# A two-thread decoder kernel: the second thread's first state-space block is prepared inside the first thread's first layer

## The chip, the core and the metric

The kernel runs on one core of a Trainium2 chip. The metric is the device time of one execution in microseconds. The core has five engines with instruction queues of their own, each worked off in order: PE (TensorE; its weight loads are listed as PEld), DVE (VectorE), ACT (ScalarE), POOL (GpSimd) and SP (SyncE, which here issues most DMAs). An instruction that waits holds up everything behind it in its engine's queue.

## The reference, cut to what matters

A decoder of 12 layers runs on x of shape (8, 256, 256), float32, each layer as `x = x + layer(layernorm(x), ...)`. The layer that the change touches is the first, a selective state-space model with a forward and a backward direction. For u after a causal convolution of four taps and a Silu it computes, per direction,

```
dbc   = u @ Wx.T                     # 64 columns dt, 16 columns B, 16 columns C
delta = softplus(dt @ Wdt.T + bdt)
h     = exp(delta * A) * h + delta * B * u      # over t, 512 channels x 16 states
y     = sum_n h * C_n + u * D
```

and then gates y with a Silu and projects it. The second layer, cross attention with 16 heads of 64 between x and a context (77 rows per batch entry), and a mixture of experts, which needs a zeroed table of slots in DRAM, follow.

## The kernel before

x is held on chip in four blocks of two batch entries each. Two threads of work share the engines: the left one takes blocks 0 and 1, the right one blocks 2 and 3, each through all 12 layers. A thread is a Python generator; `build` always advances the thread whose planned time is the smaller (`thread` adds a planned share per step, `FIRST` for the left thread's first layer), and the right thread starts at `lag`, just after the left thread's first layer. A scheduler then orders each engine's instructions, with the order of emission as priority. So the order in all queues is fixed when the program is built.

The left thread's first layer is written apart from the right's. It is `wide` (class `Wide`): it uses the buffers of both sides, and handles 512 channels of a block at once. For each of its two blocks it makes a pass in direction f and one in direction b (`way`): 16 states, each in two halves of two channel groups, so 64 scans (L829) per pass. For each of these ACT makes exp into PSUM (L825), POOL the input product db (L827), DVE the scan. For three states out of four the sum over states goes through PE transposes (L854, `ht`), an ACT scaling (L856, `ys`) and transposes back into the four sums y (L859); for every fourth state DVE multiplies by C (L832, `hc`, two buffers) and PE adds it up (L833). Between the halves `way` takes one step each from `parts`, a list of preparations: `gates` (W_in and Silu of the gate branch, L873), `channels` of the next block (norm, turn, W_in, convolution as four matmuls with diagonal `taps` and Silu, L726), `rows` (Wx matmul, copy `dbc`, store of the B and C rows to DRAM, and a small turned copy `cols`, L762), `delta` (softplus, L782) and `gated` (gate and projection of the block before, L885). In block 0's b direction the list holds all of block 1's preparation; in block 1's b direction it holds `gates` alone. Then `gated` closes the layer.

The right thread's first layer is `ssm` (L541). It loads the same weights w0 again (three DMAs, L547), and for each block normalizes and turns x, makes u (W_in, ACT copy, convolution on DVE at L565 and L569, Silu), `dbc` and `rows`. For its first block it also calls `cleared`, which zeroes the right thread's table of slots by one DMA from a zeroed tile (L902). Then it runs four passes of 32 scans (L623) per block: two channel groups at a time, both directions. Each state loads one broadcast tile `rep` (L614, 512 KB, three buffers).

Beside `ssm` the left thread runs `perceiver16`, its second layer: weights w1 (four DMAs), `joined` (norms; kv at L435), v by six matmul groups through one PSUM bank, then 8 head pairs for each batch entry with q, k, scores (`sc`, L403), softmax, transposes and `av`. SP's queue at the seam holds, in this order: w1, a context load, w0 for the right thread, the zeroes, a context load, the rows stores of block 2, the rep loads.

Of the kernel before, what the change touches and what calls it, by code (L numbers as in the profile page):

```python
# [18 lines left out]
C = 77  # L19
# [276 lines left out]
class Base:  # L296
# [22 lines left out]
    def load(self, blk):  # L319
        xd = self.d["x"].rearrange("b (i p) c -> p (b i) c", p=128)  # L320
        self.nc.sync.dma_start(self.x[blk], xd[:, 4 * blk : 4 * blk + 4, :])

    def load_rest(self):
        for blk in range(1, NB):
            self.load(blk)


class Net:
# [21 lines left out]
        self.ps = {k: pool(k, n, space=PSUM) for k, n in psum.items()}  # L350
        return es

    def weights(self, i, split=1):

        src = self.d[f"w{i}"]
        n = src.shape[1]
        m = self.d[f"r{i}"].shape[1] if f"r{i}" in self.d and src.dtype != U8 else 0
        t = self.work.tile([128, n + m], src.dtype, name=f"w{i}")
        step = -(-n // split)
        for j in range(0, n, step):  # L360
            e = min(n, j + step)
            self.nc.sync.dma_start(t[:, j:e], src[:, j:e])
# [149 lines left out]
def context(base, room, net):  # L512


    nc = net.nc
    rows = room.work.tile([C, B, D], F32, name="rows")
    nc.sync.dma_start(rows, net.d["ctx"].rearrange("b s c -> s b c"))
    yield
    for kind in ("raw", "nrm"):
        if kind == "nrm":  # L520
            net.norm([rows[:, b, :] for b in range(B)], rows, rows=C)
            yield
        dst = room.work.tile([128, 2, B * C], F32, name="turned")
# [17 lines left out]
def ssm(net):  # L541
# [2 lines left out]
    nc = net.nc  # L544
    with net.scope(mm=2, y=1):
        work = net.work
        w = net.weights(0, 3)  # L547
        neg_a, skip = {}, work.tile([128, 4], F32, name="skip")
        for d in "fb":
            e = work.tile([128, 4, 16], F32, name=f"nega_{d}")  # L550
# [2 lines left out]
            neg_a[d] = e  # L553
        nc.vector.tensor_tensor(skip, w["fD"], w["bD"], ALU.add)
        for blk in net.blks:
            xt = net.normed_turned(blk, bufs=1)
            u = work.tile([128, 4, 2, S], F32, name="u")
            for c in range(4):
                ps = net.bank()
                net.mms(ps, [(w["W_in"][:, k, c * 128 : c * 128 + 128], xt[:, k, :]) for k in range(2)])  # L560
                u0 = work.tile([128, 2, 3 + S], F32, name="u0", bufs=2)
                nc.gpsimd.memset(u0[:, :, 0:3], 0.0)
                nc.scalar.copy(u0[:, :, 3:], pairs_of(ps))
                acc = work.tile([128, 2, S], F32, name="acc", bufs=2)
                nc.vector.tensor_scalar(  # L565
                    acc, u0[:, :, 0:S], w["conv"][:, c, 0:1], w["b_conv"][:, c : c + 1], ALU.mult, ALU.add
                )
                for k in range(1, 4):
                    nc.vector.scalar_tensor_tensor(  # L569
                        acc, u0[:, :, k : k + S], w["conv"][:, c, k : k + 1], acc, ALU.mult, ALU.add  # L570
                    )
                nc.scalar.activation(u[:, c], acc, AF.Silu)
                yield
            dbc, rows = {}, {}
            for d in "fb":
                ps = net.bank()
                net.mms(pairs_of(ps[:96]), [(w[d + "Wx"][:, c, :], u[:, c]) for c in range(4)])
                dbc[d] = work.tile([96, 512], F32, name="dbc_" + d)
                nc.scalar.copy(dbc[d], ps[:96])

                rows[d] = net.base.dram.tile([32, 512], F32, name=f"rows{blk}{d}")
                nc.sync.dma_start(rows[d], dbc[d][64:96])
            if blk == net.blks[0]:
                yield from cleared(net, net)
            yield
            for c0 in range(0, 4, 2):
                y = [net.ps["y"].tile([128, 512], F32, name=f"y{c}") for c in range(2)]
                for d in "fb":
# [23 lines left out]
                    for n in range(16):  # L612
                        rep = work.tile([128, 2, 512], F32, name="rep", bufs=3)
                        nc.sync.dma_start(rep, by_state[n : n + 1].to_broadcast([128, 2, 512]))  # L614
                        for c in range(2):

                            st = net.bank()
                            nc.scalar.activation(  # L618
                                st, dl[:, c, :], AF.Exp, scale=neg_a[d][:, c0 + c, n : n + 1]
                            )  # L620
                            db = work.tile([128, 512], F32, name="db", bufs=3)
                            nc.gpsimd.tensor_tensor(db, du[:, c, :], rep[:, 0], ALU.mult)  # L622
                            nc.vector.tensor_tensor_scan(  # L623
                                st[:, order], st[:, order], db[:, order], 0.0, ALU.mult, ALU.add
                            )
                            hc = work.tile([128, 512], F32, name="hc", bufs=4)
                            nc.vector.tensor_tensor(hc, st, rep[:, 1], ALU.mult)  # L627
                            nc.tensor.matmul(  # L628
                                y[c],
                                lhsT=net.ident,  # L630
                                rhs=hc,
                                start=d == "f" and n == 0,
                                stop=d == "b" and n == 15,
                            )
                            yield
                for m in range(2):
                    c = c0 + m
                    ps = net.bank()
                    cols = slice(512 + c * 128, 640 + c * 128)
                    net.mms(ps, [(w["W_in"][:, k, cols], xt[:, k, :]) for k in range(2)])  # L640
                    res = work.tile([128, 2, S], F32, name="res")
                    nc.scalar.activation(res, pairs_of(ps), AF.Silu)
                    nc.vector.scalar_tensor_tensor(
                        u[:, c], u[:, c], skip[:, c : c + 1], pairs_of(y[m]), ALU.mult, ALU.add
                    )
                    nc.vector.scalar_tensor_tensor(u[:, c], res, 0.5, u[:, c], ALU.mult, ALU.mult)
                yield
            for b in range(2):
                net.project(blk, b, u[:, :, b], w["W_out"])
                yield  # L650


class Wide:
# [7 lines left out]

    def steps(self):
        net, nc, other = self.net, self.nc, self.other
        with net.scope(y=1), other.scope(st=2, ht=2):
            net.ps.update(other.ps)
            net.alias = {"mm": "ht"}
            near = net.work
            self.w = w = net.weights(0, 3)
            taps = near.tile([128, 4, 4, 128], F32, name="taps")
            nc.sync.dma_start(taps.rearrange("p c k m -> p (c k m)"), net.d["taps"])  # L670
            self.taps = taps
# [14 lines left out]
            for n, blk in enumerate(net.blks):  # L686
                then = {"blk": blk + 1}
                self.y = [net.ps["y"].tile([128, 512], F32, name=f"y{c}") for c in range(4)]
                for d in "fb":
                    parts = []  # L690
                    if d == "f":
# [3 lines left out]
                            parts.append(self.rows(now, "b"))  # L695
                        parts.append(self.delta(now, "b"))
                        if n == 0:
                            parts += [context(self.base, other, net)]
# [13 lines left out]
    def way(self, o, d, parts):  # L712
# [10 lines left out]
        for _ in parts:  # L723
            yield

    def channels(self, o, first=False):  # L726
# [4 lines left out]
        xt = o["xt"] = near.tile([128, 2, 512], F32, name="xt", bufs=2)  # L731
# [6 lines left out]
        u = o["u"] = near.tile([128, 4, 2, S], F32, name="u", bufs=2)  # L738
# [23 lines left out]
    def rows(self, o, d):  # L762
# [5 lines left out]
        dbc = o["dbc"][d] = near.tile([96, 512], F32, name="dbc_" + d, bufs=2)  # L768
# [1577 lines left out]
```

## Time and profile before

| | us |
|---|---|
| median of 3 runs (lowest, highest) | 4766.82 (4752.45, 4772.51) |
| profiled execution: time, span | 4753.15, 4751.4 |
| leading layer: first scan, last scan, gate | 49.2, 517.1, 520.3 |
| directions f and b of block 0, f and b of block 1, first to last scan | 107.5, 133.9, 121.5, 96.5 |
| left thread's layer 1: weights issued, first kv, first scores | 530.7, 548.8, 589.0 |
| right thread's first scan, 129th scan, last scan's start | 589.1, 977.5, 1304.8 |

The scans of each layer are counted in the timeline of DVE (64 for each direction of the left layer, 32 for each pass of the right). In a line of the timeline the first number is the start, the second the length; "x2" merges two neighbours, and brackets give the engine's idle time before it and what ended that. Line numbers are those of the listing above.

### The profile page before, as it was taken

What the parts mean: (1) busy time and instruction counts of PE and PEld (TensorE: products, weight loads), DVE (VectorE), ACT (ScalarE), POOL (GpSimd) and SP (SyncE); (2) the same over time, 40 slices, a digit from 0 to 9 for tenths busy, and PEclk for the clock granted to TensorE, in tenths of its full rate; (3) what the DMA queues carried; (4) which work ended last, traced back from release to release, by engine and by line L of the source; (5) the groups of instructions that cost most, each with busy time, mean ns of one, the idle gap of its engine ahead of it and who ended that gap; (6) DMA issues with size and microseconds to landing.
All of it is one profiled execution on the core that took longest, in us unless ns stands there. A gap on an engine that the chain in (4) does not pass through costs nothing.

```text
span 4751.4 us, 54874 instructions
## 1 busy us (share of the span) xinstructions
PE 4087.7 (86%) x20192; PEld 2663.6 (56%) x20192; DVE 2665.2 (56%) x5064; ACT 2004.2 (42%) x4513; POOL 1576.2 (33%) x1373
## 2 busy tenths in 40 slices
PE   7777788887889899988989998788989999877988
PEld 3555433433347566655766665555556767645655
DVE  6768787767841444556254556665473562243355
ACT  6767465656533343432333342422343342233331
POOL 5758454344512411124442333432011001122123
PEclk8989899988989899998989998777889999988999
DMA  3111343233416100001610000100010000001000
GB/s 125 55 33 48 117 112 101 58 90 96 99 57 235 60 1 1 13 3 71 242 42 1 1 32 16 41 14 1 1 47 1 14 36 1 34 25 40 2 18 36
DMA packets 96319, 239.72 MB, mean 50 GB/s; under 512 B 8395, under 2 KB 36403, under 8 KB 85683
## 3 DMA queue, kind: packets, MB, share of 16 engines
q1 hardware_dynamic: 86355, 179.49, 12.2%
q0 software_dynamic: 9696, 56.72, 3.4%
q8 instruction: 160, 2.62, 0.2%
q14 instruction: 108, 0.88, 0.1%
HBM read 216.05 MB, written 20.14 MB: 50 GB/s over the span
## 4 chain that ended last, share of the span: by engine, by line
PE 46%; DVE 11%; POOL 5%; issue 4%; ACT 3%; DMA 1%; POOLq 0%; DVEq 0%; ACTq 0%
PE mm L395 22%; PE sc L395 5%; PE sc L403 5%; PE av L403 3%; PE pt L395 3%; PE o L395 3%; PE mm L983 1%; DVE xn L418 1%; PE mm L403 1%; PE mm L2175 1%; PE mm L428 1%; PE mm L1840 1%; DVE hn_sq L1897 1%; DVE pex L979 1%; POOL m_part L1596 1%
## 5 line engine op out<-in xcount | busy, mean ns | idle before, releaser
L622 POOL TENSOR_TENSOR db<-du,rep 128x512 f32<-128x512 f32 x256 | 320.2, 1271 | 182.6 <-DMA rep<-rows3f 44.2
L827 POOL TENSOR_TENSOR db<-du,rep 128x512 f32<-128x512 f32 x256 | 320.9, 1284 | 105.1 <-DVE h L829 81.9
L387 ACT COPY pv<-mm 111x384 f32<-111x384 f32 (+2 forms) x387 | 197.7, 512 | 331.6 <-PE mm L983 144.6
L395 PE MATMUL mm<-xt,w 128*128 128x512 f32 (+1 forms) x704 | 310.2, 569 | 30.7 <-issue 6.2
L623 DVE TENSOR_TENSOR_SCAN mm<-mm,db 128x512 f32<-128x512 f32 x256 | 310.7, 1222 | 36.7 <-ACT mm L618 20.9
L1333 POOL TENSOR_TENSOR qs<-q,w 128x256 f32<-128x256 f32 x256 | 155.4, 628 | 479.6 <-PE sc L395 479.0
L403 PE MATMUL sc<-k,q 64*128 64x333 f32 (+1 forms) x1152 | 249.5, 492 | 74.0 <-ACT pex L970 36.1
L628 PE MATMUL y<-hc,consts 128*128 128x512 f32 x512 | 279.1, 651 | 38.0 <-DVE hc L627 37.9
L403 PE MATMUL av<-pv,v 111*64 111x256 f32 (+5 forms) x2752 | 255.6, 384 | 16.3 <-ACT pv L387 9.2
L395 PE MATMUL sc<-k,qs 128*128 128x256 f32 x1024 | 265.8, 388 | 3.4 <-ACT ex L1347 1.6
L983 PEld LDWEIGHTS mm<-consts,pex 128*111 128x111 f32 x960 | 146.2, 195 | 195.5 <-issue 52.6
L983 PE MATMUL mm<-consts,pex 128*111 128x128 f32 x960 | 197.0, 316 | 61.8 <-ACT pex L977 18.5
L829 DVE TENSOR_TENSOR_SCAN h<-st,db 128x512 f32<-128x512 f32 x192 | 223.2, 1208 | 41.4 <-ACT st L825 34.4
L395 PE MATMUL mm<-h,sw 128*128 128x256 f32 x1024 | 243.3, 384 | 0.0
L970 ACT ACTIVATE pex<-sc,pnm 128x333 f32<-128x333 f32 x320 | 170.3, 537 | 139.3 <-DVE pnm L966 122.9
L403 PEld LDWEIGHTS sc<-k,q 64*128 64x128 f32 (+1 forms) x1152 | 111.8, 200 | 195.4 <-ACT pex L970 67.9
L395 PE MATMUL mm<-kv,w 128*128 128x256 f32 (+1 forms) x640 | 207.3, 445 | 13.3 <-ACT q L1024 10.8
L416 POOL TENSOR_TENSOR rs<-ve,neghalf 128x4 f32<-128x4 f32 (+1 forms) x57 | 59.2, 1039 | 476.3 <-DVE ve L414 395.1
L395 PEld LDWEIGHTS mm<-h,sw 128*128 128x128 f32 x1024 | 192.7, 193 | 32.9 <-issue 6.9
L395 PEld LDWEIGHTS mm<-xt,w 128*128 128x128 f32 x704 | 133.6, 206 | 136.4 <-issue 82.1
L395 PE MATMUL mm<-w,ao 128*128 128x256 f32 x768 | 197.5, 398 | 12.4 <-DVE x L462 10.8
L395 PEld LDWEIGHTS sc<-k,qs 128*128 128x128 f32 x1024 | 181.7, 192 | 45.2 <-issue 15.9
(482 smaller groups left out, 9073.4 us busy)
## 6 DMA issues: line engine op xcount, KB each, us to landing
rep<-rows2f SPq DMA_DIRECT2D x32, 512.0 KB
rep<-rows2b SPq DMA_DIRECT2D x32, 512.0 KB
rep<-rows3f SPq DMA_DIRECT2D x32, 512.0 KB
rep<-rows3b SPq DMA_DIRECT2D x32, 512.0 KB
w<-in_w SPq DMA_DIRECT2D x12, 1024.0 KB
w<-in_w SPq DMA_DIRECT2D x8, 1025.0 KB
w<-in_w SPq DMA_DIRECT2D x6, 1001.0 KB
w<-in_w SPq DMA_DIRECT2D x6, 838.0 KB
```

The lines of the kernel that those rows point to most:

```text
L387: self.nc.scalar.copy(out, in_)
L395: self.nc.tensor.matmul(out, lhsT=lhs, rhs=rhs, start=n == 0, stop=n == len(pairs) - 1)
L403: self.nc.tensor.matmul(out, lhsT=lhs, rhs=rhs, start=start, stop=stop, tile_position=at)
L416: nc.gpsimd.tensor_tensor(rs[:rows], ve[:rows], self.neghalf[:rows, :n], ALU.pow)
L622: nc.gpsimd.tensor_tensor(db, du[:, c, :], rep[:, 0], ALU.mult)
L623: nc.vector.tensor_tensor_scan(st[:, order], st[:, order], db[:, order], 0.0, ALU.mult, ALU.add)
L628: nc.tensor.matmul(y[c], lhsT=net.ident, rhs=hc, start=d == "f" and n == 0, stop=d == "b" and n == 15,)
L827: nc.gpsimd.tensor_tensor(db, du[:, c, :], self.rep[:, 0], ALU.mult)
L829: nc.vector.tensor_tensor_scan(h[:, order], st[:, order], db[:, order], 0.0, ALU.mult, ALU.add)
L970: nc.scalar.activation(ex[:, e, :], sc[:, e, :NK], AF.Exp, bias=nm[:, e : e + 1], accum_out=sm[:, e : e + 1])
L983: nc.tensor.transpose(pt[:CH, j * 128 : j * 128 + 128], ex[:, e, j * CH : (j + 1) * CH], net.ident)
L1333: nc.gpsimd.tensor_tensor(qs[:, kc].rearrange("p n (h t) -> p n h t", h=H), q[:, kc, t0 : t0 + 16].rearrange("p (n t) -> p n t", n=2).unsq ...
```

## The change

Four things move together. (1) A pool `shared`, opened by the leading layer at the bottom of the right side, holds w0 and stays open until `ssm` ends, so `ssm` loads no weights. (2) In block 1's b direction the list of preparations now also holds `channels` and both `rows` of block 2, with their results in `shared`; `rows` leaves out the turned copy `cols` for it. (3) `ssm` takes these results for its first block and starts with the softplus; its second block is prepared as before. (4) `cleared` for the right thread is called after the first pass of the first block instead of ahead of it. The context rows take the buffer of `res`, since memory is needed for `shared`. `ssm` has four steps fewer, which moves the right thread's later instructions ahead by 6.5 units of the plan's 2241.

```diff
+    def hand(self):
+        self.handed = ExitStack()
+        self.shared = self.handed.enter_context(
+            self.tc.tile_pool(name="shared", bufs=1, side="right", reuse_waits="tile")
+        )
...
-    def weights(self, i, split=1):
+    def weights(self, i, split=1, pool=None):
...
-        t = self.work.tile([128, n + m], src.dtype, name=f"w{i}")
+        t = (pool or self.work).tile([128, n + m], src.dtype, name=f"w{i}")
...
-    rows = room.work.tile([C, B, D], F32, name="rows")
+    rows = net.work.tile([128, 4, 512], F32, name="res").rearrange("p a (n c) -> p (a n) c", c=D)[:C]
...
 def ssm(net):
-        w = net.weights(0, 3)
+        shared, first = net.base.shared, net.base.first
+        w = first["w"]
...
         for blk in net.blks:
+            if blk == net.blks[0]:
+                xt, u, dbc, rows = (first[k] for k in ("xt", "u", "dbc", "rows"))
+            else:
...
-            if blk == net.blks[0]:
-                yield from cleared(net, net)
             yield
             for c0 in range(0, 4, 2):
...
+                    if blk == net.blks[0] and not c0 and d == "f":
+                        yield from cleared(net, net)
...
+    net.base.handed.close()
...
 class Wide:
     def steps(self):
+        self.base.hand()
...
-            self.w = w = net.weights(0, 3)
+            self.w = w = net.weights(0, 3, self.base.shared)
...
                     else:
                         parts.append(self.gates(now))
+                        parts += [self.channels(then), self.rows(then, "f"), self.rows(then, "b")]
                         if blk != net.blks[-1]:
-                            parts += [self.channels(then), self.rows(then, "f"), self.rows(then, "b")]
                             parts.append(self.delta(then, "f"))
...
+            self.base.first = dict(now, w=w)
             self.turn(4)
...
     def rows(self, o, d):
...
         nc.sync.dma_start(rows, dbc[64:96])
         yield
+        if o["blk"] not in net.blks:
+            return
```

In the lines that are left out, `channels` and `rows` take their tiles xt, u and dbc from `shared` for a block of the other thread (one buffer) and from their own pool otherwise (two buffers), and the body of `ssm`'s preparation is indented under the `else`.

More of the change, by code (lines that the diff above doesn't have):

```diff
@@ L555, in ssm @@
         for blk in net.blks:
[L556 to L570, printed above, removed]
-                    )
-                nc.scalar.activation(u[:, c], acc, AF.Silu)
-                yield
@@ L574, in ssm @@
[L574 to L582, printed above, removed]
-            if blk == net.blks[0]:
-                yield from cleared(net, net)
+            if blk == net.blks[0]:
+                xt, u, dbc, rows = (first[k] for k in ("xt", "u", "dbc", "rows"))
+            else:
+                xt = shared.tile([128, 2, 512], F32, name="xt")
+                net.turned(net.normed(blk), [xt[:, kc, :] for kc in range(2)])
+                u = shared.tile([128, 4, 2, S], F32, name="u")
+                for c in range(4):
+                    ps = net.bank()
+                    net.mms(ps, [(w["W_in"][:, k, c * 128 : c * 128 + 128], xt[:, k, :]) for k in range(2)])
+                    u0 = work.tile([128, 2, 3 + S], F32, name="u0", bufs=2)
+                    nc.gpsimd.memset(u0[:, :, 0:3], 0.0)
+                    nc.scalar.copy(u0[:, :, 3:], pairs_of(ps))
+                    acc = work.tile([128, 2, S], F32, name="acc", bufs=2)
+                    nc.vector.tensor_scalar(
+                        acc, u0[:, :, 0:S], w["conv"][:, c, 0:1], w["b_conv"][:, c : c + 1], ALU.mult, ALU.add
+                    )
+                    for k in range(1, 4):
+                        nc.vector.scalar_tensor_tensor(
+                            acc, u0[:, :, k : k + S], w["conv"][:, c, k : k + 1], acc, ALU.mult, ALU.add
+                        )
+                    nc.scalar.activation(u[:, c], acc, AF.Silu)
+                    yield
+                dbc, rows = {}, {}
+                for d in "fb":
+                    ps = net.bank()
+                    net.mms(pairs_of(ps[:96]), [(w[d + "Wx"][:, c, :], u[:, c]) for c in range(4)])
+                    dbc[d] = shared.tile([96, 512], F32, name="dbc_" + d)
+                    nc.scalar.copy(dbc[d], ps[:96])
+                    rows[d] = net.base.dram.tile([32, 512], F32, name=f"rows{blk}{d}")
+                    nc.sync.dma_start(rows[d], dbc[d][64:96])
@@ L697, in steps @@
                         if n == 0:
-                            parts += [context(self.base, other, net)]
+                            parts.append(context(self.base, other, net))
                             parts += [cleared(Net(self.base, net.blks, side), other) for side in CLEARED]
@@ L724, in way, with of, bufs @@
             yield
+    def of(self, o):
+        return self.net.work if o["blk"] in self.net.blks else self.base.shared
+    def bufs(self, o):
+        return 2 if o["blk"] in self.net.blks else 1
     def channels(self, o, first=False):
@@ L730, in channels @@
         yield
-        xt = o["xt"] = near.tile([128, 2, 512], F32, name="xt", bufs=2)
+        xt = o["xt"] = self.of(o).tile([128, 2, 512], F32, name="xt", bufs=self.bufs(o))
         for kc in range(2):
@@ L737, in channels @@
             yield
-        u = o["u"] = near.tile([128, 4, 2, S], F32, name="u", bufs=2)
+        u = o["u"] = self.of(o).tile([128, 4, 2, S], F32, name="u", bufs=self.bufs(o))
         for c in range(4):
@@ L767, in rows @@
         net.mms(pairs_of(ps[:96]), [(w[d + "Wx"][:, c, :], o["u"][:, c]) for c in range(4)])
-        dbc = o["dbc"][d] = near.tile([96, 512], F32, name="dbc_" + d, bufs=2)
+        dbc = o["dbc"][d] = self.of(o).tile([96, 512], F32, name="dbc_" + d, bufs=self.bufs(o))
         nc.scalar.copy(dbc, ps[:96])
```

## The prediction

> **What bounds the kernel now.** I read the page's totals first, then a table of 5 us windows around the seam between the two layers, then the timeline of that seam, then the same timeline inside the leading layer, where the trace already holds a twin of the moved work.
>
> ```profile
> PE 4087.7 (86%) x20192; PEld 2663.6 (56%) x20192; DVE 2665.2 (56%) x5064; ACT 2004.2 (42%) x4513; POOL 1576.2 (33%) x1373
> ```
>
> PE is the busiest engine, but 86% is an average over stages. In the windows (columns: stretch, length, busy us of PE, PEld, DVE, ACT, POOL, granted PE clock, DMA share, GB/s) the seam is the weakest place:
>
> ```profile
> 505.00:510.00 5.00, 4.28 (x33) 3.76 (x32) 3.83 (x5) 4.81 (x9) 4.39 (x5) 0.92 0.02 3
> ...
> 525.00:530.00 5.00, 4.91 (x22) 4.02 (x23) 1.69 (x4) 0.00 (x0) 0.00 (x0) 1.00 0.00 0
> ...
> 535.00:540.00 5.00, 0.19 (x1) 0.18 (x1) 4.21 (x20) 0.00 (x0) 1.01 (x1) 0.50 0.97 392
> ```
>
> In the first row, before the leading layer ends, DVE, ACT and POOL are at 77% or more; in the second ACT and POOL stand still; in the third the DMAs are full with three transfers at once and PE's clock is granted at 0.50. The timeline says who comes back when:
>
> ```profile
> 520.29 1.41 DVE L889 SCALAR_TENSOR_TENSOR u<-u,skip,y 128x512 f32<-128x512 f32 x2 [2.03 <-PE y L859]
> 530.74 1.97 SPq L362 DMA_DIRECT2D w<-in_w  x4
> 548.84 0.81 DVE L435 TENSOR_SCALAR kv<-mm,w 128x512 f32<-128x512 f32 x1
> 588.99 1.48 PE L403 MATMUL sc<-k,q 64*128 64x333 f32 x4 [0.81 <-ACT k L387]
> 589.09 1.23 DVE L623 TENSOR_TENSOR_SCAN mm<-mm,db 128x512 f32<-128x512 f32 x1 [1.25 <-POOL db L622]
> ```
>
> The leading (left) thread needs 68.7 us from its gate (520.29) to its first score matmul (588.99), and the second (right) thread starts its first scan at the same moment (589.09). Behind that, the left thread sets the pace: the score matmuls of successive head pairs start at
>
> ```profile
> 611.59 0.83 PE L403 MATMUL sc<-k,q 64*128 64x333 f32 x4 [0.91 <-ACT k L387]
> 634.51 0.83 PE L403 MATMUL sc<-k,q 64*128 64x333 f32 x4
> ...
> 908.47 0.83 PE L403 MATMUL sc<-k,q 64*128 64x333 f32 x4
> ...
> 929.40 0.83 PE L403 MATMUL sc<-k,q 64*128 64x333 f32 x4
> ```
>
> The first gap, 22.9 us, holds 12 scans of the right thread; the second, 20.9 us, holds none. A scan of the right thread costs the left chain (22.9 - 20.9)/12 = 0.17 us, though it holds DVE for 1.22 + 0.69 us. That row decides my sign.
>
> **The change, part by part.**
>
> *Moved into the last direction (left path).* The trace has the twin: the other block's b direction prepares block 1 by the same lines 726 to 780, and in the built program the changed direction has PE's instructions in the same order. Each direction has 64 scans. Here are the 17th scan and the 49th of both, and between them the two DVE waits that the twin has:
>
> ```profile
> 181.16 2.34 DVE L829 TENSOR_TENSOR_SCAN h<-st,db 128x512 f32<-128x512 f32 x2 [0.23 <-ACT st L825]
> 218.81 0.69 DVE L832 TENSOR_TENSOR hc<-st,rep 128x512 f32<-128x512 f32 x1 [10.66 <-PE y L833]
> 260.15 0.69 DVE L832 TENSOR_TENSOR hc<-st,rep 128x512 f32<-128x512 f32 x1 [12.51 <-PE y L833]
> 262.60 1.22 DVE L829 TENSOR_TENSOR_SCAN h<-st,db 128x512 f32<-128x512 f32 x1 [1.75 <-ACT st L825]
> ...
> 443.55 2.34 DVE L829 TENSOR_TENSOR_SCAN h<-st,db 128x512 f32<-128x512 f32 x2 [0.23 <-ACT st L825]
> ...
> 495.60 2.34 DVE L829 TENSOR_TENSOR_SCAN h<-st,db 128x512 f32<-128x512 f32 x2 [0.23 <-ACT st L825]
> ```
>
> 262.60 - 181.16 = 81.4 us against 495.60 - 443.55 = 52.1 us: 29.4 us for channels and rows. (The gates stand in both, the softplus of L784 in neither.) The changed kernel leaves out the two small transpose rounds of L773 to L779, about 2 us each (249.55 to 250.4 and a bank's turn). I take **+25 us**. Upper end 37.4, the whole difference of the two directions from first scan to last (133.9 - 96.5), softplus included. Lower end 15, ACT's added instructions alone: 4 copies of 0.58, 4 Silus of 0.69, 3 copies of 0.59 and 6 table loads of 1.28 (L758 has 3, the way back to Exp 3 more) are 14.5. Nothing hides it: all four engines are at 78% to 86% in the window 405 to 520, and the wait is PE's order, in which the tap matmuls stand before y<-hc, with DVE's hc (two buffers) and everything after it in DVE's queue behind.
>
> A rule speaks against this place. The Trainium skill, "ScalarE: Activation LUTs", section "What ACT_TABLE_LOAD costs", counts about 2.66 us for every change of table set, load and drain; the six added loads would be 16 us of ACT by it. The trace has 1283 ns loads with the next ACTIVATE at once behind them (load at 240.56, Silu at 241.86), so it shows no drain after the load, and 7.7 us by its own rows.
>
> *Removed from the seam.* The right thread's weight load (3 x 838 KB, some 6.5 us of full DMA at the 392 GB/s of the window), its norm and turn, 8 W_in and 8 Wx matmuls (32 records of about 0.45 = 14.4 us of PE, at 555 to 580 where PE is full) and 4 x 0.55 + 12 x 0.75 = 11.2 us of DVE convolution. The convolution comes back as 16 tap matmuls, inside the +25.
>
> *Right thread.* Its first Abs needs only the prepared projection: PE's first Wdt matmul follows the last y turn directly. From Abs to first scan takes 589.09 - 578.51 = 10.6 us now; behind the gate's DVE work (to 525.4) I get about 533 + 25 = **558 us instead of 589**, 31 us earlier.
>
> *Left thread in the seam.* In DVE's built order 6 scans (1.22), 6 products (0.69) and the softplus (about 3) now stand before kv: 14.5 us; some is waiting now, so kv moves from 548.84 to 562 before the shift, +13. POOL's powers for the norms wait behind six db of 1.27, which is how those us come about. After kv the 14.4 us of PE are gone, less what the right thread's matmuls add: -13. PE's half clock in 535 to 555 covers 7.6 us of busy time and can give back 3.8. I take **0**, bounds -10 and +10. First left score matmul: 589 + 25 = **614**.
>
> *SP's queue.* The rows stores (64 KB each) and cleared's zeroing move. Though cleared stands later in the text, SP gets it before the left thread's layer-1 weights: three rep loads (1.5 MB) and 2.94 MB of zeros, together 1.5/0.17 + 2.94/0.39 = 16 us by the rates of the windows 580 to 585 (rep loads alone) and 535 to 540, start about 10 us before those 4.2 MB. They are needed at kv, 30 us after their issue; 6 + 11 us fit under DVE's work. Cover gone, up to 7 us. The ctx rows' new home in res costs nothing: gates needs it at 179, the last reader is done at 118.
>
> *What the lead is worth.* In the built program 17 y matmuls of the right thread stand before the first left score matmul (none now), but at the 128th scan 48 score matmuls against 52, at the 256th 108 against 112: the lead shrinks to one head pair, 21 us. Left gains 17 x 0.17 = **-3**. So at the end of the right layer (about 1305) the left thread is 22 us late and the right on time.
>
> *The rest.* From 2400 us to the end PE is busy 2083 of 2352 us, 89%. A head pair has 8.1 us of PE in its 21 us (908 to 929: scores 1.7, transposes 2.5, av 1.5, q 1.1, k 1.3), so 22 us of left backlog hold 8.5 us of PE, 9.5 at 89%. Between that and the whole 22 I take **+12**, nearer to the PE row; bounds 0 (the right thread alone ends the kernel) and 22 (the left chain does).
>
> Sum: 25 + 0 - 3 = 22 late, of which +12 stays. Against the profiled execution (span 4751.4, time 4753.15) this gives 4765. That execution is 13.7 below the median 4766.82 of the runs, so on the median I forecast **4779 us**.
>
> **Rivals.** *The right thread's lead is worth its full price (faster).* If DVE (270 of 341 us in 589 to 930) and not the left chain is the limit, 31 us of early start remain, less a little: 4737. For it: DVE and PE are both near 80%. Against: 20.9 us without scans, 22.9 with twelve. *The left delay is paid whole (slower).* One mechanism, the last direction's stalled y<-hc: its 25 to 37 us, less 3, reach the end on the left chain because PE later waits more than it works; +29 as its middle, 4796. It passes 0.5% from a stall of 27 us that is kept whole. For it: the twin's 10.66 and 12.51 us waits. Against: 89% PE. *It does not do what it says:* the right thread starts early and then waits for the left's instructions in the shared queues, ends cancel, 4767.
>
> **How the numbers follow.** Forecast 0.45, full lead 0.22, paid whole 0.25, cancelled 0.08. Own range of the forecast: 4767 to 4789. The range reaches to both rivals' prices, 4735 to 4808. Faster by over 0.5% (below 4743, what a measurement can tell): 0.20. Slower by over 0.5% (above 4791): 0.24. Within: 0.56.
>
> **What would show it.** The last scan of the leading layer near 542 instead of 517 with waits of 10 us on y<-hc; the first right scan near 558; the first left score matmul near 614; head pairs still at 21 to 23 us; the right layer's last scan near 1305. Wrong if the leading layer ends before 530, if the first left score matmul comes before 600, or if head pairs shorten by more than 1 us when fewer scans lie between them.

## The result and the profile after

The changed kernel takes 4809.82 us (median of 6 runs, 4797.78 to 4814.03), the kernel before in the same comparison 4762.14 us. The ratio is 1.0086 with a 95% interval of 1.0065 to 1.0107: about 41 us slower (31 to 51). The profiled execution of the changed kernel took 4801.52 us, its span is 4799.7.

The line of totals of the changed kernel, first part of the page:

```profile
PE 4119.8 (86%) x20224; PEld 2680.8 (56%) x20224; DVE 2665.3 (56%) x5047; ACT 1999.1 (42%) x4510; POOL 1580.9 (33%) x1373
```

PE has 32 instructions and 32.1 us more than before; DVE's time is the same to 0.1 us. The windows of the changed kernel around its seam (columns as before: stretch, length, busy us of PE, PEld, DVE, ACT, POOL, granted PE clock, DMA share, GB/s):

```profile
515.00:520.00 5.00, 4.76 (x22) 2.50 (x21) 0.00 (x0) 1.73 (x3) 1.17 (x1) 1.00 0.26 66
...
535.00:540.00 5.00, 4.06 (x35) 3.47 (x33) 4.61 (x5) 4.91 (x9) 5.00 (x5) 1.00 0.14 34
...
570.00:575.00 5.00, 3.20 (x4) 0.51 (x3) 3.39 (x8) 0.87 (x2) 3.67 (x4) 0.50 0.97 403
```

The first row is new: inside the leading layer PE is at 95% and DVE does nothing. In the second, where the kernel before was already loading, the leading layer is still at work. The third answers to the old third row, 35 us later: the DMAs full, the clock at 0.50. The timeline of the changed kernel has the marks that were shown of before, the right scan now ahead of the left thread's kv, and two waits like those of the twin:

```profile
485.94 0.69 DVE L856 TENSOR_TENSOR hc<-st,rep 128x512 f32<-128x512 f32 x1 [10.62 <-PE y L857]
...
526.63 0.69 DVE L856 TENSOR_TENSOR hc<-st,rep 128x512 f32<-128x512 f32 x1 [11.85 <-PE y L857]
...
553.84 1.41 DVE L913 SCALAR_TENSOR_TENSOR u<-u,skip,y 128x512 f32<-128x512 f32 x2 [2.03 <-PE y L883]
564.30 2.01 SPq L369 DMA_DIRECT2D w<-in_w  x4
566.63 1.20 DVE L633 TENSOR_TENSOR_SCAN mm<-mm,db 128x512 f32<-128x512 f32 x1
594.66 0.80 DVE L442 TENSOR_SCALAR kv<-mm,w 128x512 f32<-128x512 f32 x1
625.95 0.83 PE L410 MATMUL sc<-k,q 64*128 64x333 f32 x4 [0.89 <-ACT k L394]
```

| us | before | forecast | after |
|---|---|---|---|
| leading layer, last direction, first to last scan | 96.5 | 121.5 | 126.5 |
| leading layer, last scan ends | 517.1 | 542 | 550.6 |
| left thread, first kv | 548.8 | | 594.7 |
| left thread, first score matmul | 589.0 | 614 | 626.0 |
| right thread, first scan | 589.1 | 558 | 566.6 |
| right thread, last scan | 1304.8 | 1305 | 1316.0 |
| left thread, weights of layer 2 issued | 1386 | | 1417 |

The right thread does start 22.5 us earlier, and the left thread comes to its first score matmul 37 us late. The right thread's lead is gone at the last scan of its own layer (11 us late); the left thread is 31 us late there, and the time is 41 us longer.

### The profile page after: what moved, and what is told of

It is laid out like the page before. It is cut to its first block, busy times and chain, and to the rows that moved or that the text cites. A ratio compares the mean times of both kernels' runs of the same rounds, so it can differ in the third digit from the quotient of the medians.

```text
span 4799.7 us, 54908 instructions
## 1 busy us (share of the span) xinstructions
PE 4119.8 (86%) x20224; PEld 2680.8 (56%) x20224; DVE 2665.3 (56%) x5047; ACT 1999.1 (42%) x4510; POOL 1580.9 (33%) x1373
## 4 chain that ended last, share of the span: by engine, by line
PE 48%; DVE 12%; POOL 4%; issue 4%; ACT 4%; DMA 1%; POOLq 0%; DVEq 0%; ACTq 0%
PE mm L402 23%; PE sc L410 5%; PE sc L402 5%; PE av L410 3%; PE o L402 3%; PE pt L402 3%; PE mm L1007 1%; DVE xn L425 1%; PE mm L435 1%; PE mm L2199 1%; DVE hn_sq L1921 1%; PE mm L410 1%; DVE st L418 1%; ACT pv L394 1%; PE mm L1864 1%
## 5 line engine op out<-in xcount | busy, mean ns | idle before, releaser
L410 PE MATMUL sc<-k,q 64*128 64x333 f32 (+1 forms) x1152 | 273.0, 526 | 92.8 <-ACT pex L994 51.8
L402 PE MATMUL mm<-xt,w 128*128 128x512 f32 (+1 forms) x688 | 290.3, 552 | 31.0 <-DVE rope_s L1308 13.1
L410 PE MATMUL av<-pv,v 111*64 111x256 f32 (+5 forms) x2752 | 253.6, 385 | 18.2 <-ACT pv L394 10.2
L410 PEld LDWEIGHTS sc<-k,q 64*128 64x128 f32 (+1 forms) x1152 | 121.5, 214 | 219.5 <-ACT pex L994 83.9
L402 PEld LDWEIGHTS mm<-h,sw 128*128 128x128 f32 x1024 | 191.5, 192 | 32.1 <-issue 7.5
L410 PEld LDWEIGHTS av<-pv,v 128*32 128x32 f32 (+3 forms) x2752 | 123.7, 133 | 135.0 <-issue 39.4
```

The costliest lines, as they stand in the source:

```text
L402: self.nc.tensor.matmul(out, lhsT=lhs, rhs=rhs, start=n == 0, stop=n == len(pairs) - 1)
L410: self.nc.tensor.matmul(out, lhsT=lhs, rhs=rhs, start=start, stop=stop, tile_position=at)
```

## The experiments

Two theories were put on record first. A: the left thread's chain sets the end; what delays its first score matmul is paid whole, and an early start of the right thread is worth nothing. B: the time is lost behind the seam, in the order of the queues. Lines of each kernel are its own. "Last direction" is from first to last scan; "first scores" is the first score matmul. Differences in us are the measured ratio less 1, times that comparison's own median of the kernel before (4750 to 4764). Positions inside a kernel come from one profiled execution each. They scatter: block 0's direction f holds the same instructions in the same order in the changed kernel, e5_no_tables and e6_one_tap, and takes 107.5, 104.0 and 109.7 us. The last direction repeats better: where it holds the same work it takes 126.5 to 126.7 us (the changed kernel, e1_waste, e4_zero_first, e10_zero_wide).

### The moved work alone, and the lead alone

*e1_waste*: the kernel before, with block 2's preparation in the last direction as well, thrown away.

```diff
                         parts.append(self.gates(now))
+                        parts += [self.channels(then), self.rows(then, "f"), self.rows(then, "b")]
                         if blk != net.blks[-1]:
-                            parts += [self.channels(then), self.rows(then, "f"), self.rows(then, "b")]
                             parts.append(self.delta(then, "f"))
```

> The kernel before, and block 2's preparation (channels and both rows) is done in the last direction as in the change, but its results are thrown away: the second thread prepares its own block 2 again. Theory A (the left thread's chain sets the end, its delay is paid whole): the leading layer's last scan moves from 517 to about 550, the first score matmul from 589 to about 620, the time rises by 30 to 40 us. Theory B (the time is lost later, by the changed order of the queues behind the seam, and most of the leading layer's delay is absorbed): the leading layer ends at 550 as well, but the time rises by 0 to 15 us only.

Measured: last scan 551.4, first scores 623.6, ratio 1.0082 (1.0052 to 1.0112), +39 us. As A says of the size, and B is out. Both threads are late by 34.6 us here, so the run shows that the delay is paid whole, but not whose delay it is. Its first right scan stands at 623.70, 57 us later than the changed kernel's, and the two kernels cost the same; the granted clock of the two differs, though (0.909 in the mean of its runs, 0.902 in the changed kernel's), which is taken up below:

```profile
623.60 1.48 PE L403 MATMUL sc<-k,q 64*128 64x333 f32 x4 [0.81 <-ACT k L387]
623.70 1.23 DVE L623 TENSOR_TENSOR_SCAN mm<-mm,db 128x512 f32<-128x512 f32 x1 [1.25 <-POOL db L622]
```

*e8_no_prep*: the changed kernel without the moved work; block 2's xt, u, dbc and rows are constants, so its preparation is left out of the computation.

```diff
-                        parts += [self.channels(then), self.rows(then, "f"), self.rows(then, "b")]
                         if blk != net.blks[-1]:
+                            parts += [self.channels(then), self.rows(then, "f"), self.rows(then, "b")]
                             parts.append(self.delta(then, "f"))
...
+            nc.gpsimd.memset(first["u"], 0.5)
```

> The changed kernel without the moved work: block 2's xt, u, dbc and rows are constants, written at the start of the kernel, so the whole preparation of that block is left out of the computation. The second thread starts its scans at the seam as early as can be. Theory A: the leading layer's last scan is back at 517 to 521, the first score matmul at 585 to 600, the time within 12 us of the kernel before, since the lead of the right thread is worth nothing. Theory B: the rebuilt order behind the seam still costs, 15 to 40 us above the kernel before. Theory C (the right thread's early start is worth its price, and the stall hid it): 20 us or more below the kernel before.

Measured: last scan 519.4, first scores 594.4, ratio 0.9994 (0.9974 to 1.0015). The right thread's first scan comes at 535.4, 54 us earlier than before, with 40 PE instructions fewer than before, and in time it buys at most 12 us. Theory C's 20 us are excluded.

```profile
535.37 1.20 DVE L633 TENSOR_TENSOR_SCAN mm<-mm,db 128x512 f32<-128x512 f32 x1
...
594.44 0.83 PE L410 MATMUL sc<-k,q 64*128 64x333 f32 x4 [0.89 <-ACT k L394]
```

With e1_waste this says what the slowdown comes from: the work that the change moves, put into the last direction of the kernel before and nothing else, costs 39 us, and the changed kernel without it is no slower than before (it also does less: block 2's preparation is left out altogether).

*e2_keep_w0*: the kernel before, with w0 kept on chip (a pool as in the change, `weights(0, 3, shared)`), nothing prepared early.

```diff
-        w = net.weights(0, 3)
+        w = net.base.w0
```

> The kernel before, and w0 stays on chip for the second thread; nothing else of the change. Theory A: the leading layer ends as before (517), the first score matmul stays at 585 to 592, the time within 10 us of before. Theory B: the same time, unless the three weight loads that are gone let the left thread's w1 land earlier: up to 7 us faster.

Measured: last scan 519.0, first scores 578.9, ratio 0.9983 (0.9963 to 1.0004), -8 us. The first scores came 6 us earlier than expected: with the load gone the seam (from the last scan to the first scores) takes 60.0 us instead of 71.9. This is more than the early preparation gives the left thread: the changed kernel's seam, without load and preparation, takes 75.3.

### Each thread's lateness

*e11_right_late*: the kernel before, with four more loads of w0 in `ssm`, transfers alone.

```diff
         w = net.weights(0, 3)
+        for _ in range(4):
+            nc.sync.dma_start(w.t, net.d["w0"])
```

> The kernel before, with the second thread's load of w0 followed by four more whole loads of the same weights into the same tile: nothing but transfers, so that the right thread alone is late, by some 30 us, about as late as the stall makes the left thread in the changed kernel. Theory A (the left thread's chain sets the end): first right scan near 620, first score matmul between 575 and 592, time within 12 us of the kernel before. Theory F (the last to finish, which is the right thread, sets the end): 20 to 35 us slower.

The delay came out larger than meant: the first right scan is at 644.1, 55 us late, the first scores 17.7 us early:

```profile
571.29 0.83 PE L403 MATMUL sc<-k,q 64*128 64x333 f32 x4 [0.86 <-ACT k L387]
...
644.06 1.23 DVE L625 TENSOR_TENSOR_SCAN mm<-mm,db 128x512 f32<-128x512 f32 x1 [1.25 <-POOL db L624]
```

The ratio is 1.0032 (1.0015 to 1.0048), +15 us (7 to 23). Neither theory as written: the right thread, which finishes last, does not set the end (F would give 55), but 55 us of its lateness are far from free. By A's rule first scores 17.7 us early should have made this kernel 18 us faster; it is 15 us slower, so by that rule the right thread's 55 us cost 33. (3.8 us of the 17.7 lie in the leading layer, whose instructions are those of the kernel before in the same order: scatter.)

### What holds the last direction

*e6_one_tap*: one tap of four in block 2's convolution (the other three left out).

```diff
-                net.mms(pairs_of(ps), [(self.taps[:, c, k, :], u0[:, :, k : k + S]) for k in range(4)])
+                net.mms(pairs_of(ps), [(self.taps[:, c, k, :], u0[:, :, k : k + S]) for k in range(4 if blk in net.blks else 1)])
```

> The changed kernel with one tap of four in block 2's convolution (the other three are left out): 12 matmuls of about 0.43 us fewer on PE, every round trip through the ht banks kept. Theory S1: the last direction shortens by 5 us or more (121 or less). Theory S2: by under 3 us.

Measured: 117.5 instead of 126.5, in one execution; the 9 us are clear of the last direction's scatter. S1's forecast: PE's matmuls hold it.

*e7_dveconv*: block 2's convolution on DVE, accumulating in u.

```diff
-            if first and c % 2 == 0:
-                acc = self.other.work.tile([128, 2, S], F32, name="hc", bufs=2)
+            if first and c % 2 == 0 or blk not in net.blks:
+                acc = self.other.work.tile([128, 2, S], F32, name="hc", bufs=2) if first else u[:, c]
```

> The changed kernel, with block 2's convolution in the last direction on DVE (four instructions for each of four channel groups) instead of 16 tap matmuls on PE. Theory S1 (the stall is PE's order, the tap matmuls ahead of y<-hc): the waits of 10 to 12 us on y<-hc shrink, DVE has 11 us more to do, the direction takes 105 to 118 us instead of 126.5, the time falls with it to 10 to 30 us above before. Theory S2 (the stall is the round trip of every prepared group through the two ht banks, PE to ACT and back, whoever convolves): 122 to 132 us, time 35 to 50 us above before.

Measured: 121.3, between the two; first scores 617.9; ratio 1.0063 (1.0046 to 1.0081), +30 us. The four waits on y<-hc in its last direction are short now; two of them:

```profile
480.26 0.69 DVE L856 TENSOR_TENSOR hc<-st,rep 128x512 f32<-128x512 f32 x1 [0.66 <-PE y L857]
...
517.20 0.69 DVE L856 TENSOR_TENSOR hc<-st,rep 128x512 f32<-128x512 f32 x1 [1.16 <-PE y L857]
```

The waits on y<-hc sum to 4.6 us against 24.6 in the changed kernel: 20 us of waiting went, DVE got 15.2 us more to do (98.35 against 83.15 in the direction), and the direction is 5.2 us shorter, about the difference of the two. The repair was paid for on the engine that had waited.

*e5_no_tables*: the changed kernel with Exp in place of block 2's four Silus (another function), which need no change of table.

```diff
-                nc.scalar.activation(u[:, c], pairs_of(ps), AF.Silu, bias=bias)
+                nc.scalar.activation(u[:, c], pairs_of(ps), AF.Silu if blk in net.blks else AF.Exp, bias=bias)
```

> The changed kernel with Exp in place of the four Silus of block 2's channels (another function is computed there), so that the table loads around them fall away: 1283 ns each, up to 7.7 us of ACT. Theory T (the table loads stand on the path of the stall): the last direction shortens from 126.5 by 5 to 8 us. Theory S1 (PE's order holds it): by less than 3 us. By the page on activation tables, at 2.66 us a load with its drain, it would be 16 us.

Measured: 127.5, no gain; ACT lost 8 us of work in the direction, and DVE's wait on y<-hc grew instead:

```profile
523.41 0.69 DVE L856 TENSOR_TENSOR hc<-st,rep 128x512 f32<-128x512 f32 x1 [19.74 <-PE y L857]
```

*e7b_dve_no_tables*: the same Exp in e7_dveconv.

```diff
-                nc.scalar.activation(u[:, c], acc, AF.Silu)
+                nc.scalar.activation(u[:, c], acc, AF.Silu if blk in net.blks else AF.Exp)
```

> The kernel with block 2's convolution on DVE, and Exp in place of its four Silus (another function is computed there). With the tap matmuls gone from PE, ACT is the next candidate. Theory T: the direction shortens from 121.3 by 5 us or more. If DVE's 16 convolution instructions hold it now: by less than 3 us.

Measured: 117.0 instead of 121.3. 4.3 us lie between both expectations, so whether ACT or DVE is next after PE stays open.

The whole direction in one row, for five kernels (same columns). Before:

```profile
420.60:517.10 96.50, 76.06 (x431) 53.07 (x429) 82.70 (x79) 75.99 (x119) 75.02 (x64) 0.95 0.17 50
```

After:

```profile
424.10:550.60 126.50, 102.76 (x503) 63.61 (x501) 83.15 (x79) 91.21 (x136) 75.16 (x64) 0.97 0.15 43
```

One tap of four:

```profile
426.10:543.60 117.50, 94.83 (x479) 60.59 (x477) 83.31 (x79) 93.32 (x138) 75.14 (x64) 0.94 0.15 46
```

Convolution on DVE (e7_dveconv):

```profile
421.10:542.40 121.30, 94.08 (x470) 60.37 (x469) 98.35 (x95) 93.81 (x138) 77.10 (x64) 0.93 0.15 45
```

The twin, block 0's b direction in the kernel before:

```profile
158.10:292.00 133.90, 108.78 (x497) 65.95 (x496) 88.82 (x88) 98.79 (x143) 79.51 (x67) 0.94 0.14 41
```

PE's busy time over the length is 79%, 81%, 81%, 78% and 81%: the direction is about as long as PE's work in it divided by 0.8. With the convolution on DVE it is 4 us longer than that (94.08/0.8 is 117.6), so there PE is not alone in holding it. In e12_both, e7b_dve_no_tables and e5_no_tables it is 77%, 79% and 83%. The change puts 72 PE records there, 64 records of 512-column matmuls (two for each) and 8 of transposes, which cost 26.7 us of PE; 26.7/0.8 is 33, and the direction grew by 30. Exp for Silu (PE 105.75 in 127.5) takes nothing off PE and gains nothing.

### What holds the seam

*e4_zero_first*: the changed kernel with the zeroes ahead of the first pass.

```diff
                 xt, u, dbc, rows = (first[k] for k in ("xt", "u", "dbc", "rows"))
+                yield from cleared(net, net)
...
-                    if blk == net.blks[0] and not c0 and d == "f":
-                        yield from cleared(net, net)
```

> The changed kernel, with the right thread's table of slots zeroed ahead of its first pass again. Theory A: the same as the changed kernel, within 8 us (that is, 35 to 50 us above the kernel before), since the zeroes land beside DVE's norms. Theory B: if the DMA order at the seam is what costs, 7 us or more are gained or lost against the changed kernel, and the kv line (594.66 there) moves by as much.

Measured: kv 583.9, first scores 615.6, ratio 1.0048 (1.0029 to 1.0067), +23 us. A's forecast (no difference) was wrong and B's came true: part 4 of the change costs 10 us at the kv line and at the first scores, and it is paid.

*e10_zero_wide*: no zeroes in the seam at all; they are issued in the leading layer's first direction.

```diff
-CLEARED = ("left",)
+CLEARED = ("left", "right")
```

> The changed kernel, with the right thread's zeroes issued in the leading layer's first direction, beside the left thread's: the seam has no zeroes at all. In DVE's built order six right scans still stand before the left thread's kv, as in the changed kernel (with the zeroes ahead of the first pass there were two). Theory D (the seam costs because the right thread's scans and db stand in front of the left thread's norms): kv stays 43 to 45 us behind the leading layer's last scan, first score matmul 620 to 628, time as the changed kernel, 35 to 45 us above the kernel before. Theory E (the zeroes themselves in SP's queue and on the DMAs are what costs): kv 33 to 36 us behind the last scan, first score matmul 612 to 617, time 15 to 28 us above the kernel before.

Measured: last scan 557.3 (the first direction takes 111.9 instead of 107.5 us and starts 2.3 later), kv 37.2 behind it, first scores 625.0, ratio 1.0081 (1.0061 to 1.0102), +39 us. The seam lies between D and E, 7.6 us shorter than in the changed kernel; the leading layer is 6.7 us later, so first scores and time come out as D said. That the zeroes make the leading layer late is not shown: without them there the layer starts as late in e12_both (51.2 against 51.5), and the first direction alone scatters between 104.0 and 109.7 us.

The rows that separate the three, first the changed kernel on DVE just ahead of kv:

```profile
583.83 1.22 DVE L633 TENSOR_TENSOR_SCAN mm<-mm,db 128x512 f32<-128x512 f32 x1
...
588.23 0.28 DVE L421 TENSOR_SCALAR ve<-mv 128x4 f32<-128x4 f32 x2
590.54 4.20 DVE L425 TENSOR_SCALAR xn<-x,mv,rs 128x256 f32<-128x256 f32 x4 [2.03 <-POOL rs L423]
594.66 0.80 DVE L442 TENSOR_SCALAR kv<-mm,w 128x512 f32<-128x512 f32 x1
```

Then the zeroes issued early (e10):

```profile
592.34 1.22 DVE L633 TENSOR_TENSOR_SCAN mm<-mm,db 128x512 f32<-128x512 f32 x1
...
594.47 0.77 DVE L442 TENSOR_SCALAR kv<-mm,w 128x512 f32<-128x512 f32 x1
```

In the changed kernel DVE's queue holds six right scans and then the norms of the next blocks, right and left (the x4 at 590.54 belongs to block 3), ahead of the left thread's kv. In e10 the six scans stand there and those norms mostly behind kv; with the zeroes first (e4) it is two scans and those norms. From last scan to kv: 44.0, 37.2, 33.0, and 31.8 in e1_waste, where nothing of the right thread stands there. None of these runs shows a wait of kv for a DMA, so the zeroes seem to act through the order that the scheduler builds from them; no run changes that order and leaves the zeroes where they are.

### Versions meant to be better

*e12_both*: the changed kernel with the two diffs of e7_dveconv and e4_zero_first.

> The changed kernel with both repairs at once: block 2's convolution on DVE, and the zeroes ahead of the first pass. By the rule of theory A (time follows the first score matmul one for one): last scan 542, first score matmul 65 us later at 605 to 610, so 16 to 22 us above the kernel before. If the two repairs overlap, 25 us or more above.

Measured: last scan 546.8, seam 65.1, first scores 611.9, ratio 1.0027 (1.0012 to 1.0042), +13 us (6 to 20). The repairs add up (41 less 11 for the one and 18 for the other), and the kernel is still slower than before.

*e9_w0_zero_early*: e2_keep_w0 with the zeroes in the leading layer.

```diff
-            if blk == net.blks[0]:
-                yield from cleared(net, net)
...
-CLEARED = ("left",)
+CLEARED = ("left", "right")
```

> A version that may beat both: the kernel before, w0 kept on chip, and the right thread's zeroes issued in the leading layer's first direction, so that the seam's only large transfer is w1. By the rule that the end follows the first score matmul one for one: if the zeroes hold up w1 or the rows, the first score matmul comes at 570 to 576 and the time is 12 to 20 us below the kernel before; if they are hidden there (theory D), it stays at 579 and the time at 5 to 10 us below.

Measured: first scores 579.2, ratio 1.0012 (0.9991 to 1.0033): the zeroes were hidden in that seam (e2_keep_w0: 578.9), as the second case said, but the time is not below the kernel before. The leading layer starts 2.2 us later, no more than in e12_both. No version beat the kernel before by more than the measurement can tell; e2_keep_w0 comes nearest.

## Why the prediction was right or wrong

All kernels with more than one timed run, against the kernel before (first scores 589.0, first right scan 589.1). "Clock" is the mean granted clock of a kernel's runs less that of the kernel before in the same comparison (for "after" against the profiled execution before, the only one there with a clock on record). The last column is an estimate that is explained below the list.

| kernel | first scores, us | first right scan, us | time, us (95%) | clock | time at equal clock, us (estimate) |
|---|---|---|---|---|---|
| after | +37.0 | -22.5 | +41 (31 to 51) | -0.0070 | +15 |
| e10_zero_wide | +36.0 | -15.8 | +39 (29 to 48) | -0.0094 | +4 |
| e1_waste | +34.6 | +34.6 | +39 (25 to 53) | -0.0008 | +36 |
| e7_dveconv | +28.9 | -30.3 | +30 (22 to 39) | -0.0055 | +10 |
| e4_zero_first | +26.6 | -22.2 | +23 (14 to 32) | -0.0057 | +2 |
| e12_both | +22.9 | -25.8 | +13 (6 to 20) | -0.0048 | -5 |
| e8_no_prep | +5.4 | -53.7 | -3 (-12 to 7) | -0.0058 | -24 |
| e9_w0_zero_early | -9.8 | -9.8 | +6 (-4 to 16) | -0.0048 | -12 |
| e2_keep_w0 | -10.1 | -10.1 | -8 (-18 to 2) | +0.0002 | -7 |
| e11_right_late | -17.7 | +55.0 | +15 (7 to 23) | +0.0007 | +18 |

The sign and the place were right: the moved work stalls the leading layer, and the kernel is slower. The likeliest case (+12, within 0.5%) was wrong, and the price that the rival "paid whole" names is what happened, at 41 where it was priced at 29. Its reason, that the left chain carries the delay to the end, is argued and not shown (below). On the forecast's base of 4766.82 the ratio gives 4808, the upper end of its range; that the range just holds it is luck, since no sum of the prediction comes to that. Step by step:

- *Moved into the last direction, +25*: measured +30.0, inside the bounds 15 to 37.4. The twin was the right row; its full 29.4 would have been closer than the 25 taken from it. The lower bound, counted from ACT's instructions, had the wrong engine: e5_no_tables takes 8 us off ACT and the direction stays. The named cause, tap matmuls ahead of y<-hc, is right in that PE holds it (e6_one_tap, -9.0); whether by their order or by PE's sheer work is not separated, since both matmuls and waits went in the runs that shorten it. PE's own added 26.7 us were not counted in the forecast, and they give the size. The leading layer's other 3.4 us, in block 0's b direction, which the forecast had at nothing, are within the scatter of single executions: e11_right_late takes 136.6 us there with the instructions of the kernel before (133.9 before, 137.2 after).
- *The rule of the Trainium skill* ("ScalarE: Activation LUTs", section "What ACT_TABLE_LOAD costs", about 2.66 us a change): neither its 16 us nor the 7.7 us of the rows is on the path of the changed kernel; taking the switches away gained nothing (127.5 against 126.5).
- *Right thread, 558*: measured 566.6, 16.0 behind the last scan as forecast (542 to 558); late only by the layer in front of it.
- *Left thread in the seam, 0*: measured +3.4 (75.3 against 71.9), inside -10 to +10. Its parts: +13 measured as 12.3 (last scan to kv 44.0 against 31.8), -13 as 8.9 (from kv to first scores). First scores 626 instead of 614: 8.5 in the leading layer and 3.4 here.
- *SP's queue, hidden*: no wait for w1 shows, but moving the zeroes was not free: it makes 10.4 us of the first scores (e4_zero_first). This edit was priced in the wrong place.
- *Lead, -3*: from first scores (+37) to the left thread's next weights (+31) it gains 6. The price of a scan, 0.17 us, came from two gaps (the first holds 11 scans, not 12) and was too small: over the whole layer before, head pairs beside nine scans or more take 22.6 us in the mean and those beside none 19.8, which is 0.27 for each scan. In the changed kernel head pairs take 18 to 25 us. The right layer's last scan is 11 late, not on time, and not because it shares the left thread's lateness: in e8_no_prep, where the left thread is only 5 late, the right layer takes as long from first scan to last (745 us) as in the changed kernel (749), against 716 before. A right layer that starts early takes some 30 us longer, and nearly all of that in its first 128 scans (348 us in both, 315 before). The forecast too let the lead shrink in this layer, but only by the 21 us of one head pair.
- *The rest, 22 late of which 12 stays*: this is the step that failed. Nothing was absorbed in the time: +31 at the end of the left thread's layer 1, +41 at the end of the kernel. The forecast multiplied the backlog's PE work by PE's 89% load in the later stages. In the runs the time goes with the left thread's first scores as long as the right thread is early: after and e4_zero_first have the same work for PE and the same first right scan, differ by 10.4 us in the first scores, and in time by 41 against 23.

What stays open is why it is paid whole. The account that the left thread's chain alone sets the end doesn't hold for all rows: e11_right_late should be faster by it and is slower, and e2_keep_w0 and e9_w0_zero_early stand at the same first scores and first right scan to 0.3 us and differ by 14 us in time, at the edge of what their intervals tell. A rival was not tested: the granted clock. In the three series of runs of the kernel before for which clocks are on record, a run whose mean clock is 0.01 lower is 35 to 38 us longer by a straight line through the runs (for example 4738.64 us at 0.914, 4768.19 at 0.905). At 37 us for 0.01 the lower clock of the changed kernel would be 26 of its 41 us. The last column takes that off every row. It is an estimate with an uncertainty of some 10 us, and it tells another story: with both threads late (e1_waste) 36 us are left, with the left one as late and the right one early (after, e10_zero_wide) 4 to 15, and the early right thread of e8_no_prep buys 24. So the right thread's lead may well be worth something that a lower clock takes back. Whether the new order lowers the clock, or both follow from something else, these runs don't say; none holds the clock or moves the two threads apart by transfers alone, except e11_right_late.

## What to carry to other kernels

Before moving work into a stage, divide the busy time that it adds on the stage's busiest engine by that engine's share there (26.7 us of PE at 0.8), and compare with what the stage that it leaves gets shorter by: here the seam, which lost 14.4 of those PE us and a weight load, went from 71.9 to 75.3 us. Where queues hold two threads in an order fixed beforehand, don't count an early start of one thread as a gain: here 54 us of it bought at most 12 us of time, while work that made both threads 35 us late cost 39. A wait that vanishes is no gain if the work that removes it goes to the engine that waited. And when two kernels are compared whose granted clocks differ, look at what the same difference is worth between runs of one kernel before giving the time to anything else.

## What the runs showed of the hardware

Four xn on DVE (128x256, SBUF to SBUF) take 1.38 us when POOL is quiet, 4.20 us in the changed kernel at 590.54 and 3.26 us in e10 at 588.56, each time while db runs on POOL (590.47 to 594.27 there); the scans, whose operand is in PSUM, keep their 1.2 us beside db. The Trainium skill, "SBUF — State Buffer", section "SBUF: two separate sides", says that the pair of SBUF ports that DVE and GpSimd share is locked for a whole instruction by whichever of them starts first, for DVE only in its two-port modes or with two operands from SBUF; these rows fit that, and no run was made for it.

The mean granted clock over a kernel's timed runs is 0.902 in the changed kernel and 0.899 to 0.904 in the other kernels whose right thread is first at the seam (e4, e7, e8, e10, e12). It is 0.908 to 0.910 in the three series of the kernel before, 0.909 in e1, 0.910 in e2 and 0.909 in e11, where the right thread is not first, but 0.904 in e9, where it isn't either. The score matmuls of L410 take 526 ns in the mean after, those of L403 492 before. What lowers the clock is not shown.
